# Linear attention at the head of a two-layer kernel: eight products of a constant tile on TensorE before the first k product, finer first loads, and other PSUM banks for the first k and for the split's transposes

## The chip, the cores and the metric

The kernel runs on one core of one Trainium2 chip. The metric is device time in microseconds (us), the median of several executions. Before the change it is 1000.65 us (three executions, 1000.56 to 1001.5). One further execution was profiled; it took 998.07 us, and its span, from the first to the last instruction, is 996.3 us. Durations in this document come from that one execution. Where a line of the kernel is meant, it is written L467 and so on.

TensorE (PE in the profile) multiplies matrices and writes to PSUM, which has eight banks of 128 x 512 f32 here. PEld is the loading of its stationary operand. VectorE is DVE, ScalarE is ACT, GpSimd is POOL, SyncE is SP. "PEq", "SPq" and "ACTq" are the queues in which an engine's instructions, or its DMA issues, stand.

## What is computed

Four blocks run one after the other on 2048 rows of 512 values: a linear attention, a gated feed-forward layer with 4-bit weights, a gated linear attention in chunks, and a feed-forward layer on the rows that a router picks. Each ends in a residual sum and a layer norm. The change is in the first, and in the hand-over to the second:

```python
q = elu(x @ Wq.T) + 1
k = elu(x @ Wk.T) + 1
v = x @ Wv.T                                   # 16 heads of 32
kv = einsum('bhtd,bhte->bhde', k, v)
z = 1.0 / (einsum('bhtd,bhd->bht', q, k.sum(axis=2)) + 1e-06)
out = einsum('bhtd,bhde,bht->bhte', q, kv, z)
x = layernorm(x + out @ Wo.T)
```

## The kernel before

**Tiling.** The 2048 rows are four blocks of 512 (`blk` 0 to 3), two for each of the two sequences (`b`). A block is four row tiles of 128, and the 512 channels are four chunks of 128 (`KC = 4`). All operands of this part are f32; each f32 matmul shows in the trace as two records, so that 16 matmuls of 512 columns are "x32".

**The first k product** (L462 to L470). Four banks, `first[0]` to `first[3]`, collect the k of the four row tiles of block 0. The loop goes over the channel chunk outside and the row tile inside, so that work can begin when the first chunk of `Wk` and of the transposed x has landed. For this the loads at L138 to L141 are issued in chunks: SP issues four loads of `Wk`, ACT five of `x0T`, of which chunk 0 comes in two halves of 256 tokens. Then `elu1` (L265) turns each bank into k: two ACT instructions (L270, L271) that write a buffer `e`, of which there are two, and one DVE instruction (L272) that reads the bank a second time. The bank is free after this last one.

**The other seven products** (`by_seven`, L300). Each later block of k or q is made by a scheme of seven smaller products. It takes one bank from the ring "sum", called `grow`, in which several products accumulate, and two banks from the ring "mm". `by_seven` is a generator; `run` (L480) puts other work between its products: `add_xk` (k transposed times x, which holds four banks of the ring "acc"), `values` and `G_rows` (which turn that into the matrix G), `turned` (a transposed tile of q), `add_o` (that tile times G, added to x by DVE at L448), and for the second sequence `split_some`.

**The split.** `split_quarter` (L207) transposes one normalized row tile of block 0 on TensorE (L196) into a bank, from which ACT copies a rounded part `x1Th` (L210) and DVE subtracts to get the rest `x1Tl` (L211). These are the operands of the second block's first product, `gatep` and `upp` (L621). There are four quarters. The first three come between the products of the last q, the fourth after them, before the last four `add_o`.

**Banks.** `bank(ring, name)` (L88) hands out a ring's banks in turn and counts the turns in `turn_of`. A bank is given again only when its readers are done. To begin with "mm" is banks 0 to 3 and "acc" banks 4 to 7. After the first k product "mm" becomes banks 0 and 1, and "sum" banks 2 and 3 (L471). The ring "acc" serves `add_xk`, `G_rows`, `turned`, `add_o` and the split's transposes.

**Order.** Each engine works through its queue in order. The framework orders the instructions of an engine by when it expects them to be ready, with the program's order behind that; `tc.issue_after(x)` holds what stands in it behind x. `behind()` with `last_pe` (L281 to L285) keeps the matmuls of this part in the program's order. The tile `ones` (L279) is filled by POOL and read much later by `spread_ksum` (L383).

Of the kernel before, what the change touches and what calls it, by code (L numbers as in the profile page):

```python
# [21 lines left out]
P = 128  # L22
B, T, C = 2, 1024, 512
NB = 4
KC = C // P
# [48 lines left out]
def body(ctx: ExitStack, tc: tile.TileContext, a: dict, out: bass.AP):  # L74
    nc = tc.nc
# [7 lines left out]
    dram = ctx.enter_context(tc.tile_pool(name="dram", bufs=1, space=DRAM))  # L83


    rings, turn_of = {"mm": range(4), "acc": range(4, 8)}, {"mm": 0, "acc": 0, "sum": 0}

    def bank(ring, name):  # L88
        i = rings[ring][turn_of[ring] % len(rings[ring])]
        turn_of[ring] += 1  # L90
        return psum.tile([P, 512], F32, tag=f"bank{i}", name=name)

    def mm_bank(name):
        return bank("mm", name)
# [13 lines left out]
    def place_w(i, name):  # L108
        return wpool.tile([P, KC, C], F32, tag=f"A{i}", name=name)

    Wq, Wk, Wv, Wo = (place_w(i, name) for i, name in enumerate(("Wq", "Wk", "Wv", "Wo")))
# [10 lines left out]
    def new_xT(blk):  # L122
        t = xT_slot(blk % 2, f"x0T{blk}")
        return t, a["xT"][:, blk * 512 : (blk + 1) * 512].rearrange("(k p) t -> p k t", p=P)

    def load_xT(blk):
        t, src = new_xT(blk)
        nc.sync.dma_start(out=t, in_=src)
        return t
# [6 lines left out]

    t, src = new_xT(0)
    for k in range(KC):  # L138
        nc.sync.dma_start(out=Wk[:, k], in_=a["WkT"][k * P : (k + 1) * P, :])
        for half in ((slice(0, 256), slice(256, 512)) if k == 0 else (slice(0, 512),)):  # L140
            nc.scalar.dma_start(out=t[:, k, half], in_=src[:, k, half])  # L141
    xT = {0: t}
    load_x(0)
    xT[1] = load_xT(1)
# [47 lines left out]
    def transposed(x, name, room=mm_bank):  # L192

        pt = room(name)
        for k in range(KC):
            ins = nc.tensor.transpose(pt[:, k * P : (k + 1) * P], x[:, k * P : (k + 1) * P], ident).ins  # L196
        last_turned[0] = ins
        return pt

    def split_tiles(blk):  # L200

        i, j = ((2, 2), (1, 0), (0, 1), (2, 2))[blk]
        hi = xT_slot(i, "x1Th", F32R)
        lo = wpool.tile([P, KC, 512], F32R, tag=f"A{j}", name="x1Tl")
        return hi, lo

    def split_quarter(parts, blk, i, room=mm_bank):  # L207
        hi, lo = (t[:, :, i * P : (i + 1) * P] for t in parts)
        pt = transposed(x_t[blk][:, i], "x1Tp", room).rearrange("p (k t) -> p k t", k=KC)
        nc.scalar.copy(hi, pt)  # L210
        nc.vector.tensor_sub(lo, pt, hi.bitcast(F32))  # L211
# [65 lines left out]


    ones = wk.tile([P, P], F32, name="ones", bufs=1)  # L279
    nc.gpsimd.memset(ones, 1.0)  # L280
    last_pe = [None]  # L281

    def behind():

        return ExitStack() if last_pe[0] is None else tc.issue_after(last_pe[0])  # L285

    def new_pair(name):
        return wk.tile([P, 2, C], F32, tag="kq", name=name, bufs=3)
# [3 lines left out]
    def sums_of_weights(w, rooms):  # L292

        B11, B12, B21, B22 = (w[:, 2 * e : 2 * e + 2, 256 * o : 256 * o + 256] for e in range(2) for o in range(2))
        T1, T2, T4 = rooms
        for dst, x, y in ((T1, B12, B11), (T2, B22, T1), (T4, B21, T2), (B12, B22, B12)):
            nc.vector.tensor_sub(dst, x, y)
        return T1, T2, B12, T4
# [54 lines left out]
    tile_of = lambda i: slice(i * P, (i + 1) * P)  # L353
# [49 lines left out]
    vkm_of, qT, parts = {}, {}, []  # L403
# [24 lines left out]
    def turned(blk, i):  # L428
        with behind():
            pt = transposed(pairs_of["q", blk][i // 2][:, i % 2], "qTp", acc_bank)  # L430
        last_pe[0] = last_turned[0]
        t = qT[blk, i] = wk.tile([P, KC, P], F32, tag="qT", name="qT")
        nc.scalar.copy(t.rearrange("p k t -> p (k t)"), pt)

    def add_o(blk, i):

        ao = acc_bank("ao")
        with behind():
            for k in range(KC):
                ins = nc.tensor.matmul(  # L440
                    ao, qT[blk, i][:, k], G_of[blk // 2][:, k], start=k == 0, stop=k == KC - 1
                ).ins
        last_pe[0] = ins
        x = x_t[blk][:, i]
        if i == 0:
            mv_of[blk] = sp.tile([P, 4, 2], F32, tag="mv", name="mv")
        mv = mv_of[blk]
        nc.vector.tensor_add(x, ao, x)  # L448
        row_stats(mv[:, i], x)
        if i == 3 and blk < NB - 1:  # L450
            layernorm(x_t[blk], mv, by=nc.gpsimd)

    def split_some(*part):
        if 0 in part:
            parts.extend(split_tiles(0))
        for i in part:
            with behind():
                split_quarter(parts, 0, i, acc_bank)
            last_pe[0] = last_turned[0]


    pairs_of["k", 0] = [new_pair(f"k{t}") for t in range(2)]  # L462
    first = [mm_bank("kp") for _ in range(4)]
    with behind():
        for k in range(KC):
            for i in range(4):
                ins = nc.tensor.matmul(  # L467
                    first[i], xT[0][:, k, tile_of(i)], Wk[:, k], start=k == 0, stop=k == KC - 1
                ).ins
    last_pe[0] = ins  # L470
    rings["mm"], rings["sum"] = (0, 1), (2, 3)  # L471
    Ts = {"k": sums_of_weights(Wk, slices(Tk, 0, 3))}
    for i in range(4):
        elu1(pairs_of["k", 0][i // 2][:, i % 2], first[i])
# [5 lines left out]
    def run(products, *others):  # L480

        others = list(others)
        for _ in products:
            for step in others.pop(0):
                step()
        for more in others:
            for step in more:
                step()

    def some_xk(blk, *part):  # L490
        return [lambda i=i: add_xk(blk, i) for i in part]

    def turns(blk, *part):
        return [lambda i=i: turned(blk, i) for i in part]

    def some_o(blk, *part):
        return [lambda i=i: add_o(blk, i) for i in part]
# [3 lines left out]
    def k_products(blk):  # L501
        return by_seven(xT[blk], Wk, Ts["k"], S_rooms, pairs_of.setdefault(("k", blk), []), lambda t: sum_k(blk, t))

    def q_products(blk):
        return by_seven(xT[blk], Wq, Ts["q"], S_rooms, pairs_of.setdefault(("q", blk), []), lambda t: weigh(blk, t))
# [3 lines left out]
    for b in range(B):  # L509
        i, j = 2 * b, 2 * b + 1  # L510
        if b:
            run(
                k_products(i),
                turns(1, 0, 1),
                some_o(1, 0) + turns(1, 2) + job(1) + some_o(1, 1) + turns(1, 3) + job(1),
                some_o(1, 2) + job(1), some_o(1, 3) + job(1), job(2),
            )
        run(k_products(j), [], some_xk(i, 0, 1) + job(2), some_xk(i, 2) + job(1), some_xk(i, 3) + job(1), job(1 + b))
        if b == 0:
            Ts["q"] = sums_of_weights(Wq, slices(wdn, 0, 3))  # L520
        else:

            Tq = place_w(1, "Tq")
            for n in range(3):
                nc.scalar.copy(Tq[:, n], wdn[:, n])
            Ts["q"] = (*slices(Tq, 0, 2), Ts["q"][2], *slices(Tq, 2, 3))
            S_rooms[0] = pieces_of(Tq[:, 3])
        run(
            q_products(i), [],
            some_xk(j, 0, 1) + job(1), some_xk(j, 2) + step(spread_ksum, b) + job(1), some_xk(j, 3) + job(1 + b),  # L530
        )
        if b == 0:
            xT[2] = load_xT(2)
        split = [step(split_some, n) if b else [] for n in range(4)]
        run(
            q_products(j),
            step(values, b),
            turns(i, 0, 1) + job(1 - b),
            step(G_rows, b) + split[0] + job(1 - b),
            some_o(i, 0) + turns(i, 2) + split[1] + some_o(i, 1) + turns(i, 3) + job(1 - b),  # L540
            some_o(i, 2) + split[2] + some_o(i, 3),
        )
        if b == 0:
            xT[3] = load_xT(3)
    for more in turns(3, 0, 1) + split[3] + some_o(3, 0) + turns(3, 2) + some_o(3, 1) + turns(3, 3) + some_o(3, 2, 3):
        more()
    late = mv_of[3]
# [17 lines left out]
    free = iter([1, 2, 0] * 4)  # L565
# [27 lines left out]
    with tc.tile_pool(name="s2", bufs=1) as wk2:  # L593
# [198 lines left out]
        for blk in range(NB):  # L792
            h = Hidden(blk)
            for f in range(NI):
# [23 lines left out]
                with tc.issue_after(mm) if blk or f else ExitStack():  # L818
                    mm, st = scaled_sums(f, parts, gate, up, by_three, quarter)
                sl = nc.scalar.activation(gate, gate, AF.Silu).ins  # L820
                hm = nc.gpsimd.tensor_mul(h.chunk(f), up, gate).ins  # L821
                with tc.issue_after(mm), tc.issue_after(st), tc.issue_after(hm), tc.issue_after(sl):
# [7 lines left out]
                    if blk and f in (1, 4, 7):  # L830
                        take(pieces, {1: 22, 4: 32, 7: 24}[f])
                        mm = last_p[0]
# [3 lines left out]
            parts = coming  # L836
# [604 lines left out]
    for blk in range(NB):  # L1441
# [3 lines left out]
        else:  # L1445
            o_sum(blk)
            _, scored = finish(blk - 1)
# [42 lines left out]
    _, xs = fetch(0)  # L1490
# [83 lines left out]
```

## Time and profile before

| what | us |
|---|---|
| median of three executions | 1000.65 |
| the profiled execution | 998.07 |
| its span | 996.3 |
| PE busy in the span | 972.5 |
| DVE busy in the span | 681.1 |
| PE busy in 0 to 250 | 239.87 |
| PE busy in 250 to 500 | 249.93 |
| PE busy in 500 to 750 | 246.85 |
| PE busy in 750 to 1000 (the span ends at 996.3) | 235.83 |
| first matmul starts at | 4.57 |
| first `grow` product starts at | 22.84 |
| fourth quarter of the split starts at | 229.74 |
| second block's first product starts at | 247.28 |

The start times are counted from the start of the span. A row of the waits view gives an instruction group, what ended its engine's idle time, and that time's total, count and longest piece in us. In the timeline a row gives start, duration, engine, line, operation, tiles and, in brackets, the idle time before it and what ended it.

### The profile page before, as it was taken

To read this page: it belongs to the slowest core of one execution; us is meant where nothing else is said; L and a number is where in the kernel's file an instruction comes from. 1 tells how busy PE (TensorE), PEld (TensorE's weight loads), DVE (VectorE), ACT (ScalarE), POOL (GpSimd) and SP (SyncE) were. 2 spreads that over 40 slices of the span, in tenths; PEclk is the share of its full clock that TensorE was granted. 3 is DMA by queue.
4 is the path that set the end of the run, shared out by engine and by line. 5 is a ranking of instruction groups with operands and counts; after the bars stand their busy time and mean duration, and the time that the engine had idled before them with its cause. 6 is when DMAs were issued, how large, how long until landed. Compare 5 with 4: busy or idle time off the path is not lost.

```text
span 996.3 us, 11402 instructions
## 1 busy us (share of the span) xinstructions
PE 972.5 (98%) x4229; PEld 741.8 (74%) x4229; DVE 681.1 (68%) x1290; ACT 288.7 (29%) x490; POOL 302.6 (30%) x277
## 2 busy tenths in 40 slices
PE   7999999998999999999999999999999999999996
PEld 3667666764888888888889665676778688888885
DVE  3558867865995576676664365666798795689644
ACT  2344332342562254245240333122220124220000
POOL 2020363003777445575557022102023012000022
PEclk9999999999999999999999999999999999999999
DMA  9612212200000000000010410000004302140011
GB/s 344 203 47 88 74 62 66 61 1 1 1 1 1 1 1 1 2 11 1 1 58 27 163 59 1 1 1 1 1 22 141 134 11 75 43 169 1 1 43 42
DMA packets 25690, 48.84 MB, mean 49 GB/s; under 512 B 4652, under 2 KB 6316, under 8 KB 25123
## 3 DMA queue, kind: packets, MB, share of 16 engines
q1 hardware_dynamic: 22995, 42.85, 12.9%
q0 software_dynamic: 1920, 4.22, 1.1%
q10 hardware_dynamic: 720, 1.05, 0.3%
q8 instruction: 33, 0.54, 0.2%
q14 instruction: 22, 0.18, 0.1%
HBM read 39.70 MB, written 10.52 MB: 50 GB/s over the span
## 4 chain that ended last, share of the span: by engine, by line
PE 83%; issue 8%; DVE 5%; POOL 2%; ACT 2%; DMA 0%; POOLq 0%; DVEq 0%; ACTq 0%
PE P L668 12%; PE yp L1318 9%; PE hp L1239 9%; PE gatep L621 8%; PE upp L621 8%; PE xk L362 6%; PE ao L440 5%; PE grow L311 5%; PE P L311 3%; PE ao L1122 3%; PE go L1078 2%; PE kp L467 1%; PE lp L584 1%; PE P L677 1%; PE up L995 1%
## 5 line engine op out<-in xcount | busy, mean ns | idle before, releaser
L180 POOL TENSOR_TENSOR rs<-rs,table 128x4 f32<-128x4 f32 (+1 forms) x21 | 18.9, 902 | 328.4 <-DVE rs L179 328.2
L632 DVE SCALAR_TENSOR_TENSOR gate<-gatep,scale,gate 128x512 f32<-128x512 f32 x123 | 91.3, 743 | 7.5 <-PE gatep L621 5.9
L632 DVE SCALAR_TENSOR_TENSOR up<-upp,scale,up 128x512 f32<-128x512 f32 x112 | 83.0, 741 | 0.3
L621 PE MATMUL gatep<-x1Th,wgu 128*128 128x512 f32 x176 | 73.0, 415 | 0.1
L621 PE MATMUL upp<-x1Th,wgu 128*128 128x512 f32 x176 | 69.7, 396 | 0.0
L621 PE MATMUL gatep<-x1Tl,wgu 128*128 128x512 f32 x176 | 69.5, 395 | 0.0
L621 PE MATMUL upp<-x1Tl,wgu 128*128 128x512 f32 x176 | 69.5, 395 | 0.0
L821 POOL TENSOR_TENSOR h<-up,gate 128x512 f32<-128x512 f32 x30 | 38.6, 1288 | 75.9 <-ACT gate L820 70.9
L626 ACT ACTIVATE gate<-gatep,scale 128x512 f32<-128x512 f32 x41 | 28.3, 691 | 113.4 <-PE gatep L621 104.6
L668 PE MATMUL P<-wdn,h 128*128 128x256 f32 x256 | 60.5, 379 | 0.0
L440 PE MATMUL ao<-G,qT 128*128 128x512 f32 x128 | 58.7, 605 | 0.6 <-ACT x1Th L210 0.6
L1122 PE MATMUL ao<-W1o,uT 128*128 128x512 f32 x128 | 55.6, 592 | 0.0
L668 PEld LDWEIGHTS P<-wdn,h 128*128 128x128 f32 x256 | 48.5, 190 | 6.7
L1026 POOL TENSOR_TENSOR sum<-sum,sq 128x512 f32<-128x512 f32 x12 | 19.3, 1606 | 107.6 <-issue 83.7
L1122 PEld LDWEIGHTS ao<-W1o,uT 128*128 128x128 f32 x128 | 24.0, 190 | 28.7 <-issue 27.5
L440 PEld LDWEIGHTS ao<-G,qT 128*128 128x128 f32 x128 | 24.3, 195 | 25.9 <-issue 25.6
L187 DVE BATCH_NORM_STATS2 st<-x 128x6 f32<-128x512 f32 x64 | 42.7, 682 | 0.8
L362 PE MATMUL xk<-pair,x 128*128 128x512 f32 x96 | 42.7, 592 | 0.0
L621 PEld LDWEIGHTS upp<-x1Th,wgu 128*128 128x128 f32 x176 | 33.0, 188 | 9.3 <-DVE up L632 1.1
L621 PEld LDWEIGHTS gatep<-x1Th,wgu 128*128 128x128 f32 x176 | 33.1, 188 | 7.7 <-PE x1Tp L196 0.3
L621 PEld LDWEIGHTS upp<-x1Tl,wgu 128*128 128x128 f32 x176 | 33.1, 188 | 7.5
L621 PEld LDWEIGHTS gatep<-x1Tl,wgu 128*128 128x128 f32 x176 | 33.1, 188 | 7.2 <-issue 0.2
(403 smaller groups left out, 2231.6 us busy)
## 6 DMA issues: line engine op xcount, KB each, us to landing
pk<-in_gu SPq DMA_DIRECT2D x16, 352.0 KB, 3.7
x<-in_x SPq DMA_DIRECT2D x4, 1024.0 KB, 12.8
w<-in_w SPq DMA_DIRECT2D x1, 4096.0 KB, 14.4
xs<-picked SPq DMA_DIRECT2D x4, 1024.0 KB, 5.1
out<-x SPq DMA_DIRECT2D x4, 1024.0 KB, 4.3
w<-in_w SPq DMA_DIRECT2D x4, 1024.0 KB, 7.6
x0T<-in_xT SPq DMA_DIRECT2D x3, 1024.0 KB, 6.9
pk<-in_dn SPq DMA_DIRECT2D x11, 256.0 KB, 3.4
```

The source lines that it names most:

```text
L187: nc.vector.bn_stats(st, x)
L311: ins = nc.tensor.matmul(ps[:, 256 * r : 256 * r + 256], a[:, k, r * P : (r + 1) * P], b[:, k], start=first and r == 0 and k == 0, stop=k ...
L362: ins = nc.tensor.matmul(acc_of[b][c], x_t[blk][:, i, c * P : (c + 1) * P], pairs_of["k", blk][i // 2][:, i % 2], start=blk % 2 == 0 and i ...
L440: ins = nc.tensor.matmul(ao, qT[blk, i][:, k], G_of[blk // 2][:, k], start=k == 0, stop=k == KC - 1).ins
L621: ins = nc.tensor.matmul(ps, wgu[:, k, at * P : (at + 1) * P], x[:, k], start=x is parts[0], stop=x is parts[1]).ins
L626: nc.scalar.activation(acc, ps, AF.Copy, scale=s)
L632: last = nc.vector.scalar_tensor_tensor(acc, ps, s, acc, ALU.mult, ALU.add).ins
L668: last_p[0] = nc.tensor.matmul(cut, x(j)[:, r], w[:, j], start=j == 0, stop=j == NP - 1 and tail is None).ins
L821: hm = nc.gpsimd.tensor_mul(h.chunk(f), up, gate).ins
L1122: nc.tensor.matmul(ao[i], uT[blk][:, k, i * P : (i + 1) * P], W1o[:, k], start=n == 0, stop=n == 3)
L1239: nc.tensor.matmul(ps[:, 256 * j : 256 * j + 256], w[:, k, 2 * g + j], x[:, k], start=k == 0, stop=k == 1)
L1318: nc.tensor.matmul(ps[:, 256 * r : 256 * r + 256], x(r, j), w(j), start=j == 0, stop=j == NJ - 1)
```

## The change

The first chunk of `Wk` is loaded in two halves of 256 output channels, and the first chunk of `x0T` in parts of 128, 128 and 256 tokens. DVE fills `ones` in place of POOL. Eight 128 x 128 products of `ones` with itself are put on TensorE into one bank of the ring "acc"; nothing reads them, and the first k product is kept behind them. The first k product uses banks 4, 5, 1 and 3 in place of 0, 1, 2 and 3, and for chunk 0 each of its matmuls is two of 256 columns. After it, the turns of the ring "mm" begin at 0 again. The first three quarters of the split take the "sum" bank that the last q's `grow` does not use, in place of a bank of the ring "acc", and the fourth quarter takes a bank of the ring "mm".

```diff
-    rings, turn_of = {"mm": range(4), "acc": range(4, 8)}, {"mm": 0, "acc": 0, "sum": 0}
+    rings, turn_of = {"mm": range(4), "acc": range(4, 8)}, {"mm": 0, "acc": 0, "sum": 0, "free": 0}
...
     for k in range(KC):
-        nc.sync.dma_start(out=Wk[:, k], in_=a["WkT"][k * P : (k + 1) * P, :])
         for half in ((slice(0, 256), slice(256, 512)) if k == 0 else (slice(0, 512),)):
-            nc.scalar.dma_start(out=t[:, k, half], in_=src[:, k, half])
+            nc.sync.dma_start(out=Wk[:, k, half], in_=a["WkT"][k * P : (k + 1) * P, half])
+        for part in ((slice(0, 128), slice(128, 256), slice(256, 512)) if k == 0 else (slice(0, 512),)):
+            nc.scalar.dma_start(out=t[:, k, part], in_=src[:, k, part])
...
     ones = wk.tile([P, P], F32, name="ones", bufs=1)
-    nc.gpsimd.memset(ones, 1.0)
-    last_pe = [None]
+    nc.vector.memset(ones, 1.0)
+
+    idle = bank("acc", "idle")
+    for _ in range(8):
+        ins = nc.tensor.matmul(idle[:, :P], ones, ones, start=True, stop=True).ins
+    last_pe = [ins]
...
             with behind():
-                split_quarter(parts, 0, i, acc_bank)
+                split_quarter(parts, 0, i, lambda name: bank("free", name))
...
     pairs_of["k", 0] = [new_pair(f"k{t}") for t in range(2)]
+    rings["mm"] = (4, 5, 1, 3)
     first = [mm_bank("kp") for _ in range(4)]
     with behind():
         for k in range(KC):
             for i in range(4):
-                ins = nc.tensor.matmul(
-                    first[i], xT[0][:, k, tile_of(i)], Wk[:, k], start=k == 0, stop=k == KC - 1
-                ).ins
+                for o in (slice(0, 256), slice(256, 512)) if k == 0 else (slice(0, 512),):
+                    ins = nc.tensor.matmul(
+                        first[i][:, o], xT[0][:, k, tile_of(i)], Wk[:, k, o],
+                        start=k == 0 and o.start == 0, stop=k == KC - 1, skip_group_check=True,
+                    ).ins
     last_pe[0] = ins
-    rings["mm"], rings["sum"] = (0, 1), (2, 3)
+    rings.update(mm=(0, 1), sum=(2, 3))
+    turn_of.update(mm=0)
...
         split = [step(split_some, n) if b else [] for n in range(4)]
+        rings["free"] = (rings["sum"][(turn_of["sum"] + 1) % 2],)
         run(
             q_products(j),
...
+    rings["free"] = rings["mm"]
     for more in turns(3, 0, 1) + split[3] + some_o(3, 0) + turns(3, 2) + some_o(3, 1) + turns(3, 3) + some_o(3, 2, 3):
         more()
```

## The prediction

> **What bounds the kernel now.** I read the page's busy times first, then all waits of TensorE, then the chain that ended last for the first 300 us, and then the timeline around each wait.
>
> ```profile
> PE 972.5 (98%) x4229; PEld 741.8 (74%) x4229; DVE 681.1 (68%) x1290; ACT 288.7 (29%) x490; POOL 302.6 (30%) x277
> ```
>
> TensorE has work in 98% of the span, so nearly all of the remaining time is in its few waits. The waits view names the ones that the change can touch:
>
> ```profile
> PE kp L467 <- DMA x0T<-in_xT: 4.6, 1, 4.6
> PE x1Tp L196 <- DVE x1Tl L211: 2.6, 1, 2.6
> PE grow L311 <- DVE k L272: 2.3, 1, 2.3
> PE ao L440 <- ACT x1Th L210: 0.6, 1, 0.6
> ```
>
> The reader is to see that these are four single events, not repeated ones. Between 24.84 and 215.40 the chain is TensorE alone, piece after piece, so a microsecond won at the start arrives at 215 whole. The waits show only half of the loss, though. The timeline of the weight loads shows TensorE's pace, since each load follows the record before it:
>
> ```profile
> 7.29 0.34 PEld L467 LDWEIGHTS kp<-Wk,x0T 128*128 128x128 f32 x1 [0.52 <-issue]
> 8.14 0.34 PEld L467 LDWEIGHTS kp<-Wk,x0T 128*128 128x128 f32 x1 [0.52 <-issue]
> 8.80 0.19 PEld L467 LDWEIGHTS kp<-Wk,x0T 128*128 128x128 f32 x1 [0.32 <-issue]
> 9.23 0.19 PEld L467 LDWEIGHTS kp<-Wk,x0T 128*128 128x128 f32 x1 [0.24 <-issue]
> ...
> 232.87 0.34 PEld L440 LDWEIGHTS ao<-G,qT 128*128 128x128 f32 x1 [0.52 <-issue]
> 233.72 0.27 PEld L440 LDWEIGHTS ao<-G,qT 128*128 128x128 f32 x1 [0.52 <-issue]
> 234.22 0.19 PEld L440 LDWEIGHTS ao<-G,qT 128*128 128x128 f32 x1 [0.24 <-issue]
> ```
>
> Starts lie 0.855 us apart up to 8.14 and 0.43 apart from 8.80. The step of 0.66 between holds 0.46 at the slow pace, so the change of pace is at about 8.6. The same slow pace is there again after the wait at 229.74, and ends at about 233.9. Around that second wait the timeline reads:
>
> ```profile
> 226.87 0.24 PE L552 MATMUL pg<-table,sg 88*128 88x88 f32 x1
> 229.06 0.63 DVE L211 TENSOR_TENSOR x1Tl<-x1Tp,x1Th 128x512 fp32r<-128x512 f32 x1
> 229.74 0.66 PE L196 MATMUL x1Tp<-table,x 128*128 128x128 f32 x4 [2.63 <-DVE x1Tl L211]
> 230.20 0.68 DVE L448 TENSOR_TENSOR x<-ao,x 128x512 f32<-128x512 f32 x1
> 231.03 5.08 PE L440 MATMUL ao<-G,qT 128*128 128x512 f32 x8 [0.63 <-ACT x1Th L210]
> 235.94 0.60 PE L196 MATMUL qTp<-table,pair 128*128 128x128 f32 x4
> ```
>
> Quarter 3 of the split stands in the bank of quarter 2, whose subtraction DVE reaches only at 229.06, although ACT copied it at 222.77: DVE is busy without a gap from 218.46. Then the product takes 4.91 us to the next start, where the same eight records take 3.43 elsewhere in the chain.
>
> **What the Trainium skill says.** "TensorE: Matmul & The Clock Gate", Part 1 (The HAM clock gate): TensorE runs at half rate by default and after idling, and goes to full rate after a busy window of about 3.4 us; the window is free-running. The trace agrees: the pace halves exactly, and 8.6 and 233.9 are 66.0 windows of 3.413 us apart. "PSUM — Partial Sum Buffer", PSUM bank collisions, asks to guard PSUM by bank, not by address; so a late reader holds the whole bank, as at 229.74. The same page, The four PSUM rules, says that a first matmul clears a bank's accumulate bits as a whole, so the two halves of chunk 0 need one `start` only; no trace here shows it. "DMA: Bandwidth & Descriptors", Issuing engines are not separate DMA queues: SP's and ACT's loads share the engines and interleave. The trace agrees: 0.75 of all DMA time is in use in 2 to 4 us with both issuing.
>
> **Part 1, the front.** The first product now needs 128 x 256 of Wk and 128 x 128 of x: with the interleaved neighbour part some 256 KB. DMA windows of 0.25 us before (74, 29, 147, 266, 299, 291 GB/s and so on from 1.75) sum to 276 KB at 3.25 and 512 KB at 4.1. Before, both queues' first 256 KB were needed, and the release came at 4.53, 0.4 after that point; so now the data should be there at about 3.7. But the eight products stand ahead. They can start at 0.71 (POOL's memset start) + 0.20 (its duration) + 0.05 = 0.96. No row shows a 128-column f32 product at the slow pace. Nearest is vk (L412): 32 records, 16 products, in 3.57 us, 0.223 each; twice that for the slow pace is 0.446, and eight are 3.57. They end at 4.53. So the start is won not at all (4.53 against 4.57), and the smaller loads are hidden behind the products. The clock is what is won: with windows where they lay before, 1.77 to 5.19 is now a busy one, and the slow pace ends at 5.19. It costs (5.19 - 4.53)/2 = 0.33 in place of (8.6 - 4.57)/2 = 2.0. Gain 1.7. Bounds: if a half-busy window suffices, the products go faster and data decides: 0.87 + 2.0 = 2.9. If the loads and streams of the products don't overlap (0.34 + 0.21 each at the slow pace, half after 5.2), they end at about 7.6: a loss of 1.0. I take 1.7 since loads overlap in vk.
>
> Chunk 0 as 16 records of 256 columns in place of 8 of 512: the `P` row of L311 takes 1.73 for 8, 0.216 each, so nothing is added; the extra loads (0.19, or 0.34 slow) lie beside records as long as they. SP and ACT each issue one DMA more (0.42 and 0.46). Before, ACT's fifth and SP's fifth DMA waited until 4.5 and 4.35, as if eight could be in flight; now the third and fourth chunks fall under this wait. With 5 to 6.6 us to landing they are there at about 10; chunk 2 is used at 4.53 + 0.3 + 2 x 3.43 = 11.7 and chunk 3 at 15.1. Hidden; without that cover a microsecond each. x of block 0, which queues on SP behind them (landing 17.2 before), is first used at 22. The memset costs DVE 0.2 while it has nothing else.
>
> **Part 2, the first k's banks.** The last kp record starts at 19.96 (its group ends at 20.55, and a record's latency is 0.592), and `grow` could follow at 20.39. It waits to 22.84 for bank 2, until DVE has made k of row tile 2. Its successor starts at 24.68, and without the wait at 20.39 + 1.73 = 22.12. Gain 2.5. Afterwards bank 2 and bank 0 are unused, so both products follow at once. What is late next: add_xk, 3.46 after kp's end, needs k of tiles 0 and 1 (0.2 and 0.8 after it, from 20.71 and 21.31 against 20.55) and banks 4 to 7, of which 4 and 5 come free by the same two instructions. xT of block 1 landed at 14.6; `grow` now comes at about 18.7. The DVE sum of Wq at 22.70 needs a load that lands at about 21.6 and may hold back k of tile 3; its reader comes some 17 us later. Bounds 2.3 to 2.6.
>
> **Part 3, the split's banks.** Quarter 3 goes to bank 1, last read at 219.06 (L346), and may follow pg at 227.0. Its four transposes take 0.43. The ring "acc" is shifted by one for the unread products and loses the splits' turns, so add_o of tile 0 gets the bank of block 2's tile 2, read at 224.35. It starts at 227.41 at full pace and ends at 230.84. The next transpose's bank was block 2's tile 3, whose read (L448) begins at 230.20 and ends at 230.88; it starts at 230.93 in place of 235.94. Gain 5.0: 2.63 + 0.63 waits, 1.5 slow pace, 0.2 slow transposes. Quarters 0 to 2 share one bank, with 4 us and more from a subtraction to the next quarter. What is late next is that read, by 0.1 only. Bounds: without the second slow pace in an ordinary execution (the window falls differently) 3.5; with the DVE read behind the fourth subtraction and row statistics (0.69 + 0.69 + 0.18) about 3.4; 5.1 at best.
>
> **Sum.** 1.7 + 2.5 + 5.0 = 9.2 us. From the profiled 998.07 that gives 988.9; the span falls from 996.3 to 987.1. The median lies 2.6 above the profiled time, which I keep: 1000.65 - 9.2 = 991.5. After 242 the second block is bound by TensorE and its operands are ready, so nothing gives this back.
>
> **Rivals.** (a) The wait at the split moves rather than goes: DVE is the bound from 218 to 231, and its order there may change. For: no gap in its timeline, 0.1 slack. Against: its old order suffices. With a gain of 2 there: 994.5. (b) The eight products don't bring the clock up in time, or run longer than estimated. For: window position is free, and no trace shows such products. Against: TensorE is busy without a gap from 0.96. With no gain in part 1: 993.2. (c) The slower side: DVE's in-order queue puts the memset behind the first sums of the weights and of xT (5.42 to 16.6). Then the products run from 16.8 to 20.4, kp ends at 34.1, and `grow` comes 11.3 late; less 5.0 at the split: 1007. It decides once the memset ends after 10.3, where a loss of 7.5 in the front eats parts 2 and 3. Against: POOL's memset was ordered to 0.71, ahead of copies that wait for the table. (d) Other bank numbers later (the rings are rebuilt at L788 and L843) shift small waits by a microsecond or two, either way.
>
> **How the numbers follow.** The forecast has 0.55; its own range is 990 to 993. (a) has 0.17, (b) 0.15, (c) 0.03, (d) with larger losses than said 0.10, of which half still ends under 998.6. A measurement of this kernel can tell 0.2%, about 2 us, from no change. So faster 0.92, same 0.05, slower 0.03. The range 989.3 to 996.3 takes in (a), (b) and the bounds of parts 1 and 3.
>
> **What would show it.** Right: products from about 1.0 to 4.5, kp's records at 0.43 by 5 to 7 us, no wait before the first `grow`, no wait over 0.5 at the split's fourth quarter and no record pace of 0.855 around 231; the second block's first product at about 238. Wrong: a late memset, first kp well after 4.6, or a new wait of TensorE on L448 or L211 near 222 to 230.

## The result and the profile after

The changed kernel takes 989.44 us in the median of four executions (988.88 to 990.65), against 1001.01 us for the kernel before beside it (four executions, among them the three of 1000.65). The ratio is 0.9886, with a 95% interval of 0.9869 to 0.9903. The profiled execution went from 998.07 to 988.88 us, its span from 996.3 to 987.1 us.

Lines of the changed kernel are numbered a few higher: L474 is L467 before, L316 is L311, L197 is L196, L212 is L211, L445 is L440 and L453 is L448; in some experiments they shift by a few more.

In the view of all waits, these are TensorE's in the changed kernel (waiter, line, releaser; then us in total, count, longest):

```profile
PE dp L989 <- DVE last L974: 1.5, 2, 1.2
PE ep L942 <- ACT l L931: 1.3, 1, 1.3
PE hp L1250 <- ACT row L1218: 1.1, 1, 1.1
PE idle L285 <- DVE ones L281: 1.0, 1, 1.0
PE rp L1163 <- DVE score L1146: 0.9, 1, 0.9
PE kp L474 <- DMA x0T<-in_xT: 0.3, 1, 0.3
PE mp L1043 <- POOL sum L1037: 0.3, 1, 0.3
```

The three waits of the attention part (x1Tp 2.6, grow 2.3, ao 0.6) are gone, and the wait for the first data is 1.0 for the constant tile instead of 4.6 for x. One wait is new: kp for x, 0.3. The others belong to later stages and were there before with the same sizes.

The timeline of TensorE in the changed kernel at the start:

```profile
1.04 3.64 PE L285 MATMUL idle<-ones 128*128 128x128 f32 x16 [1.04 <-DVE ones L281]
4.51 1.89 PE L474 MATMUL kp<-Wk,x0T 128*128 128x256 f32 x8
6.73 12.29 PE L474 MATMUL kp<-Wk,x0T 128*128 128x256 f32 x32 [0.33 <-DMA x0T<-in_xT]
18.86 1.89 PE L316 MATMUL grow<-Wk,x0T 128*128 128x256 f32 x8
20.59 1.89 PE L316 MATMUL P<-Wk,x0T 128*128 128x256 f32 x8
```

kp begins at 4.51, right behind the eight products (the listed end of a group overlaps the start of the next, here as in other rows), and kp's first eight records, of 256 columns, take 1.73 us at full pace before the wait. The new wait stands before the other 32: row tiles 2 and 3 need the third part of x. `grow` follows kp at once, and so does `P`, the second product of `by_seven`. And around the split's fourth quarter:

```profile
222.78 0.60 PE L197 MATMUL x1Tp<-table,x 128*128 128x128 f32 x4
223.22 3.67 PE L445 MATMUL ao<-G,qT 128*128 128x512 f32 x8
...
224.97 0.63 DVE L212 TENSOR_TENSOR x1Tl<-x1Tp,x1Th 128x512 fp32r<-128x512 f32 x1
...
226.11 0.68 DVE L453 TENSOR_TENSOR x<-ao,x 128x512 f32<-128x512 f32 x1
...
226.85 0.66 PE L197 MATMUL qTp<-table,pair 128*128 128x128 f32 x4
```

The fourth quarter starts at 222.78, although the third's subtraction only starts at 224.97. The next transpose, at 226.85, comes right behind the read at 226.11 to 226.79: now that read is the last to arrive, with next to no wait.

A reckoning by starts, in the two profiled executions:

| place | before | after | won in all | won in this part |
|---|---|---|---|---|
| end of kp, where `grow` could start | 20.39 | 18.86 | 1.53 | 1.5 (front) |
| second product of by_seven | 24.68 | 20.59 | 4.09 | 2.6 (first k's banks) |
| transpose after the fourth quarter | 235.94 | 226.85 | 9.09 | 5.0 (split's banks) |
| span | 996.3 | 987.1 | 9.2 | |

So the profiled gain is 9.2 us and comes from where the prediction had put it. But the median fell by 11.6. Two questions were left: which part carries the missing 2.4 us, and why x came late in kp.

### The profile page after: what moved, and what is told of

Read it like the earlier page. It is cut to its first block, busy times and chain, and to the rows that moved or that the text cites. A ratio compares the mean times of both kernels' runs of the same rounds, so it can differ in the third digit from the quotient of the medians.

```text
span 987.1 us, 11453 instructions
## 1 busy us (share of the span) xinstructions
PE 972.1 (98%) x4253; PEld 745.1 (75%) x4253; DVE 683.3 (69%) x1291; ACT 288.4 (29%) x490; POOL 300.2 (30%) x276
## 4 chain that ended last, share of the span: by engine, by line
PE 84%; issue 8%; DVE 4%; POOL 2%; ACT 1%; DMA 1%; POOLq 0%; ACTq 0%; DVEq 0%
PE P L679 12%; PE yp L1329 9%; PE hp L1250 9%; PE gatep L632 8%; PE upp L632 8%; PE ao L445 6%; PE xk L367 6%; PE grow L316 5%; PE P L316 4%; PE ao L1133 3%; PE go L1089 2%; PE lp L595 1%; PE P L688 1%; PE kp L474 1%; PE up L1006 1%
## 5 line engine op out<-in xcount | busy, mean ns | idle before, releaser
L445 PE MATMUL ao<-G,qT 128*128 128x512 f32 x128 | 57.3, 593 | 0.0
L445 PEld LDWEIGHTS ao<-G,qT 128*128 128x128 f32 x128 | 23.8, 190 | 24.3 <-issue 23.9
```

What stands on the lines that cost most here:

```text
L445: ins = nc.tensor.matmul(ao, qT[blk, i][:, k], G_of[blk // 2][:, k], start=k == 0, stop=k == KC - 1).ins
```

## Experiments

Four kernels first, each the changed one with one part undone.

### The split's banks undone

```diff
-                split_quarter(parts, 0, i, lambda name: bank("free", name))
+                split_quarter(parts, 0, i, acc_bank)
```

> The changed kernel with the split's transposes back in the ring acc. Theory (the split's bank holds TensorE, and the idle time also halves its pace): the wait of x1Tp on DVE x1Tl of about 2.6 us is back at the fourth quarter, with some records 0.855 apart behind it; the distance from the last q's side product to the second block's first product is 3.3 to 5.0 us longer than in the changed kernel (5.0 if the pace halves, 3.3 if not), so a span of 990.4 to 992.1. Rival (the gain at the split came from the earlier order of DVE, not from the bank): no wait over 1 us there, span 987 to 988.5.

Measured: median 995.89 us (993.13 to 996.54), ratio to before 0.9958 (0.9943 to 0.9972), profiled span 993.9. The span is above the expected one since kp had a wait of 2.0 us for x in this execution; `grow` came at 20.37. At the split, TensorE's timeline and then its weight loads:

```profile
227.17 0.66 PE L197 MATMUL x1Tp<-table,x 128*128 128x128 f32 x4 [2.63 <-DVE x1Tl L212]
...
228.50 0.50 PE L632 MATMUL gatep<-x1Th,wgu 128*128 128x512 f32 x1 [0.68 <-ACT x1Th L211]
228.84 5.29 PE L445 MATMUL ao<-G,qT 128*128 128x512 f32 x8
...
233.97 0.60 PE L197 MATMUL qTp<-table,pair 128*128 128x128 f32 x4
```

```profile
229.27 0.29 PEld L445 LDWEIGHTS ao<-G,qT 128*128 128x128 f32 x1 [0.24 <-issue]
230.07 0.34 PEld L445 LDWEIGHTS ao<-G,qT 128*128 128x128 f32 x1 [0.52 <-issue]
230.93 0.34 PEld L445 LDWEIGHTS ao<-G,qT 128*128 128x128 f32 x1 [0.52 <-issue]
...
232.63 0.24 PEld L445 LDWEIGHTS ao<-G,qT 128*128 128x128 f32 x1 [0.52 <-issue]
233.11 0.19 PEld L445 LDWEIGHTS ao<-G,qT 128*128 128x128 f32 x1 [0.24 <-issue]
```

The wait is back at its old size, 2.63, and behind it the records are 0.855 us apart for some 3.4 us. The transpose comes at 233.97; with the front's 1.51 taken off it is 5.6 later than in the changed kernel, of which some 0.6 is work that stands earlier in the order here (`pg` and the first `gatep`). The rival, an earlier order of DVE, falls.

### The first k's banks undone

```diff
-    rings["mm"] = (4, 5, 1, 3)
+    rings["mm"] = (0, 1, 2, 3)
```

> The changed kernel with the first k product in banks 0 to 3 again. Theory: grow waits for DVE's third k instruction, 2.3 us again, and its successor comes 2.5 us later than in the changed kernel; span about 989.6. Rival (with the front's other edits the bank is free sooner, or add_xk would have waited anyway): under 1.5 us, span under 988.6.

Measured: median 993.79 us (992.44 to 994.46), ratio to before 0.994 (0.9916 to 0.9964), span 992.2. That is 5.1 us of span, not 2.5. The timeline of TensorE shows why:

```profile
22.14 3.17 PE L316 MATMUL grow<-Wk,x0T 128*128 128x256 f32 x8 [2.34 <-issue]
25.10 2.42 PE L316 MATMUL P<-Wk,x0T 128*128 128x256 f32 x8
27.36 1.02 PE L367 MATMUL xk<-k,x 128*128 128x512 f32 x2
```

The wait is 2.34 (the view names no releaser; DVE's third k instruction runs from 21.35 to 22.04). But `grow` and `P` take 2.96 and 2.26 to the next start where 1.73 is usual, so 1.8 us are lost to half pace, for a wait of the same size that had no such sequel in the profile of before. The granted clock that the trace records agrees: from 22 to 26 it is 0.59 here and 1.00 in the profile of before. The front cost another 0.8 here: kp's first eight records took 2.42 in place of 1.89, and then it waited 0.47 for x.

### No products, and the old loads

```diff
-    for _ in range(8):
-        ins = nc.tensor.matmul(idle[:, :P], ones, ones, start=True, stop=True).ins
-    last_pe = [ins]
+    last_pe = [None]
```

> The changed kernel without the eight unread products, finer loads kept. Theory (the products only bring the clock up, and hide the finer loads): the first k record starts at 3.2 to 3.8, runs at 0.43 for each half record (half pace) until 3.4 to 6.8 us after it, and the first grow comes 0.6 to 2.4 us later than in the changed kernel, so 19.5 to 21.3. Rival (the finer loads are what wins, the products cost as much as they bring): grow within 0.4 us of 18.86, or earlier.

Measured: median 990.64 us (990.44 to 990.87), ratio 0.9912 (0.989 to 0.9935). TensorE's timeline begins with kp:

```profile
3.56 3.78 PE L472 MATMUL kp<-Wk,x0T 128*128 128x256 f32 x8 [3.56 <-DMA x0T<-in_xT]
7.68 12.57 PE L472 MATMUL kp<-Wk,x0T 128*128 128x256 f32 x32 [0.34 <-DMA x0T<-in_xT]
```

The first eight records take 3.78 at half pace, a wait of 0.34 for x follows, and `grow` comes at 20.09, as expected. So the finer loads do bring the first data a microsecond earlier, and the slow pace eats it. The products were worth 1.2 us against this profile of the changed kernel; against its second profile, shown further below, in which `grow` comes at 20.33, they were worth nothing.

```diff
-            nc.sync.dma_start(out=Wk[:, k, half], in_=a["WkT"][k * P : (k + 1) * P, half])
-        for part in ((slice(0, 128), slice(128, 256), slice(256, 512)) if k == 0 else (slice(0, 512),)):
+        nc.sync.dma_start(out=Wk[:, k], in_=a["WkT"][k * P : (k + 1) * P, :])
+        for part in ((slice(0, 256), slice(256, 512)) if k == 0 else (slice(0, 512),)):
```

> The changed kernel with the first chunk's loads as before (Wk whole, x in two halves of 256 tokens), products kept. Theory (the finer loads are hidden behind the products): first k record at 4.5 to 4.7 and grow within 0.3 us of 18.86; the 0.33 us wait for x at 6.4 is smaller or gone, since its second half is issued earlier. Rival (finer loads carry part of the gain): grow 0.5 us or more later than 18.86.

Measured: median 989.01 us (988.42 to 989.55), ratio 0.9897 (0.9874 to 0.9919), span 986.8. TensorE's timeline has one piece for kp, with no wait:

```profile
1.04 3.62 PE L284 MATMUL idle<-ones 128*128 128x128 f32 x16 [1.04 <-DVE ones L280]
4.63 14.02 PE L473 MATMUL kp<-Wk,x0T 128*128 128x256 f32 x40
18.49 1.89 PE L315 MATMUL grow<-Wk,x0T 128*128 128x256 f32 x8
```

`grow` comes 0.37 us sooner than at 18.86, a little outside the expected 0.3 and on the other side from the rival. The finer loads are not merely hidden; between these two executions they cost 0.4 us.

### Is it the idling that halves the pace?

Here the kernel before keeps its loads, its banks and both waits; only, TensorE multiplies `ones` in the waits.

```diff
+    def fill(i, n):
+        ps = psum.tile([P, 512], F32, tag=f"bank{i}", name="fill")
+        for _ in range(n):
+            with behind():
+                last_pe[0] = nc.tensor.matmul(ps[:, :P], ones, ones, start=True, stop=True).ins
+
+    fill(7, 10)
     rings["mm"], rings["sum"] = (0, 1), (2, 3)
...
         for i in part:
+            if i == 3:
+                fill(1, 12)
             with behind():
```

> The kernel before, with unread 128-column products of ones put into its two later waits: ten (about 2.2 us at full pace) in front of the first grow and twelve (2.6 us) in front of the split's fourth quarter; loads, banks and front as before. Theory (a wait of some 2.6 us costs a second time, because the pace halves for up to 3.4 us after it in those executions where a clock window falls into it): the waits stay in size, but no records 0.855 us apart behind 20 us; the profiled span is 1.0 to 2.5 us shorter than the 996.3 of before, the median 1 to 3 us below that of the kernel before, and the executions lie closer together than the 4 us of before. Rival (slow records at 231 are due to their operands or banks, not to idling): the slow records stay, median within 0.5 us of before or later.

Measured: median 996.87 us (996.17 to 997.88), against 1000.44 (997.52 to 1001.54) for the kernel before beside it; ratio 0.9967 (0.9954 to 0.9979). The profiled span, 996.0, is a miss against the expected 1.0 to 2.5 below 996.3: this execution ran at half pace until about 10.5 at its start, in place of 8.6, which puts kp's end and everything up to the split 1.0 us later. The waits kept their size: `grow` comes 2.46 after kp's end (2.45 before), released by DVE's k, and the fourth quarter again comes right behind DVE's subtraction.

```profile
23.85 1.59 PEld L311 LDWEIGHTS grow<-Wk,x0T 128*128 128x128 f32 x8 [0.26 <-DVE k L272]
...
230.75 0.66 PE L196 MATMUL x1Tp<-table,x 128*128 128x128 f32 x4
...
232.04 3.67 PE L440 MATMUL ao<-G,qT 128*128 128x512 f32 x8 [0.55 <-ACT x1Th L210]
```

The wait of `ao` behind the quarter is still there (0.55), and its eight records take 3.67 in place of 5.08, which wins 1.4. From 230 to 234 the granted clock is 1.00; in the profile of before it is 0.57. (At the start of every profile it reads 1.00, although the records there run at half pace, so for the start only the distance of the records counts.) The median fell by 3.6, more than the expected 1 to 3, and the executions lie 1.7 apart against 4.0. The rival, operands or banks, falls.

This bears on the median. The spans of the kernel before that were taken beside the experiments lie in two groups. Beside the first four kernels, seven are 995.8 to 996.9 us with a mean granted clock of 0.996, and five are 998.5 to 1000.0 with 0.993 or 0.994. A mean lower by 0.003 over 1000 us is 6 us at half pace, or 3 us lost, which is the distance of the groups. This reckoning is rough, since the mean also counts the end of the span, where the clock is at half behind TensorE's last record and costs nothing (from about 991.6 in the profile of before). The profile of the kernel before, 996.3 at 0.996, is one of the first group. No profile of the second group was kept; that its lost time lies behind the two waits is inferred from the fillings, which took it away. How many executions fall into the second group differs between sets, so the median of the kernel before is 998.64, 999.76, 1000.44 or 1001.01.

The same question at the split alone, with the loads of the best kernel below:

```diff
         for i in part:
+            if i == 3:
+                fill = psum.tile([P, 512], F32, tag="bank1", name="fill")
+                with behind():
+                    for _ in range(12):
+                        last_pe[0] = nc.tensor.matmul(fill[:, :P], ones, ones, start=True, stop=True).ins
             with behind():
-                split_quarter(parts, 0, i, lambda name: bank("free", name))
+                split_quarter(parts, 0, i, acc_bank)
```

> The loads of the kernel with x in two halves, the split's transposes in the ring acc as before, and twelve unread products of ones in front of its fourth quarter. The wait stays, only TensorE doesn't idle in it. Theory (the split's bank costs about 3.3 us of waiting and the rest, 1.5 to 3, by the halved pace): median 3.0 to 4.0 us above the kernel with x in two halves, no records 0.855 apart near 230. Rival (the wait alone costs all of it): 5 to 6.5 us above.

Measured: median 992.87 us (991.91 to 993.19), 3.8 above the same kernel with the free bank (989.05, below); spans 990.1 and 986.7, 3.4 apart. Undone without the filling it had cost 5.4 to 6.4 in the median, against 990.52 and 989.44 for the two sets of the changed kernel. So at the split the wait is worth 3.4 to 3.8. The rest, 1.6 to 3.0, is put down to pace: the traces show 1.4 to 1.7 of it in one execution, and what lies above that rests on comparing sets that were not taken beside each other.

### How many products, and which parts of x

```diff
-    for _ in range(8):
+    for _ in range(4):
```

> The changed kernel with four unread products in place of eight; they end at about 2.8 us, and data for the first k is there at about 3.6. Theory (a window has to be busy nearly in full): the first k records start at 3.5 to 3.8 at half pace, and the pace doubles at 4.4 to 7.5 us; grow at 18.5 to 20.5. Rival (half a window of work suffices): full pace at the latest by 5 us in each such execution, grow no later than in the changed kernel but for the wait for the third part of x.

Measured: median 990.24 us (988.95 to 990.77), ratio 0.9896 (0.9877 to 0.9915). The products end at about 2.8, kp starts at 3.57, and its eight records take 3.75: half pace until 7 us at least, in spite of the work from 1.04 on. So here work with a gap of 0.45 us before kp did not bring the pace up in time, and `grow` came at 20.26. That only unbroken work raises it does not follow. Without the products, above, the pace rose at about 8.2, close behind an idle gap of 0.34 at 7.34 to 7.68: from 7.68 to `grow` it took 12.41 us, where the changed kernel takes 12.13 from the same record, and 0.28 lost is 0.56 at half pace. How much idling is too much stays open.

```diff
-        for part in ((slice(0, 128), slice(128, 256), slice(256, 512)) if k == 0 else (slice(0, 512),)):
+        for part in ((slice(0, 128), slice(128, 512)) if k == 0 else (slice(0, 512),)):
```

> The changed kernel with the first chunk of x in two parts, 128 and 384 tokens, in place of 128, 128 and 256. Theory (the third part lands late because the ACT queue, with rows of 512 bytes against 1 and 2 KB on the SP queue, gets the smaller share of the DMA engines, and because it is issued a place later): the rest of x lands before 6.4, no wait over 0.2 us in kp, grow at 18.3 to 18.6. Rival (the landing is set by the total of bytes in flight, whatever the parts): a wait of 0.3 to 2 us again, in front of row tile 1 or 2.

Measured: median 990.28 us (988.9 to 991.07), ratio 0.9896 (0.9877 to 0.9915). Neither came out. kp waited 0.60 for x already before its first record, at 5.42, and the half pace went on until about 9, again with a gap in the work; `grow` came at 21.12.

```diff
-        for part in ((slice(0, 128), slice(128, 256), slice(256, 512)) if k == 0 else (slice(0, 512),)):
+        for part in ((slice(0, 256), slice(256, 512)) if k == 0 else (slice(0, 512),)):
```

> The changed kernel with the first chunk of Wk in halves but the first chunk of x in two halves of 256 tokens, as before. Same question: theory gives no wait over 0.2 us in kp and grow at 18.3 to 18.6, rival a wait of 0.3 to 2 us in front of row tile 2.

Measured: median 988.44 us (988.33 to 988.73), ratio 0.9882 (0.9865 to 0.99), no wait in kp, `grow` at 18.32. Only x differs from the changed kernel. The changed kernel and this one again, beside each other on one chip:

> The changed kernel once more, beside the next two on one chip, to have another of its executions. Theory (its finer loads of x cost a wait that differs from one execution to the next): a wait of 0.3 to 2 us for x in kp in this profile too, executions 1.5 us or more apart. Rival (the one profile was an exception): no such wait, and a median within 0.3 us of the kernel with x in two halves.

> The kernel with Wk's first chunk in halves and x in two halves of 256 tokens, against the changed kernel on the same chip. Theory: no wait in kp, median 0.5 to 1.5 us below the changed kernel, executions within 1 us. Rival: equal.

Measured: the changed kernel 990.52 us (989.49 to 990.87; ratio 0.9906, 0.9889 to 0.9924), with x in two halves 989.05 (988.31 to 989.78; ratio 0.9894, 0.9874 to 0.9914), beside 999.76 for the kernel before. Of the changed kernel's two expected signs, the wait came and the spread did not reach 1.5. With halves the median lies 1.5 lower, as expected, but the executions, expected within 1 us, also lie 1.5 apart. So a wait that differs between profiles is shown, and a smaller spread with halves is not. The timelines of TensorE, first of the changed kernel, then with two halves:

```profile
4.62 2.90 PE L474 MATMUL kp<-Wk,x0T 128*128 128x256 f32 x8
8.20 12.29 PE L474 MATMUL kp<-Wk,x0T 128*128 128x256 f32 x32 [0.68 <-DMA x0T<-in_xT]
20.33 1.89 PE L316 MATMUL grow<-Wk,x0T 128*128 128x256 f32 x8
```

```profile
4.51 13.92 PE L474 MATMUL kp<-Wk,x0T 128*128 128x256 f32 x40
18.27 1.89 PE L316 MATMUL grow<-Wk,x0T 128*128 128x256 f32 x8
```

In this second profile the changed kernel's kp begins at half pace, then waits 0.68, and `grow` comes at 20.33, against 18.86 in the first. Whenever x began with a part of 128 tokens (rows of 512 bytes), kp waited for x at least once after TensorE had begun, 0.3 to 2.0 us in all seven profiles. In the four profiles with products and halves of 256 it did not, but for a weight load that waited 0.16 us in the kernel with the old loads. The guess that the ACT queue gets the smaller share of the DMA engines with short rows did not hold for the kernel with two parts, and the traces speak against it: from 3 to 5 us all DMA engines together moved 128 to 230 GB/s in those seven profiles, and 299 to 328 GB/s in the six with halves, the kernel before and its filled form among them. So it is the whole flow that is slower then, not ACT's share of it. Why stays open.

## Why the prediction was right, and where it was not

**Part 2, the first k's banks.** Predicted 2.5, measured 2.56 in the profiles. k of the first tiles and banks 4 and 5 were in time, as said. In ordinary executions it is worth more: undoing it cost 3.3 to 4.4 us of median, against the two sets of the changed kernel, and its profile shows 1.8 of half pace beside the wait.

**Part 3, the split's banks.** Predicted 5.0, measured 5.0, in an execution before that had one slow stretch at the split. The next to arrive late is the read by L453 that the prediction named, within 0.1 us. The second block's first product on the new quarters came at 238.12, where about 238 had been forecast. The bound "without the second slow pace in an ordinary execution (the window falls differently) 3.5" fits the wait alone, 3.4 to 3.8. What it did not weigh right is the other direction: ordinary executions of the kernel before lose more to half pace than the profiled one.

**Part 1, the front.** Predicted 1.7, measured 1.5 in the profile, by other terms. The products did end at about 4.5 and the first record did start there. The pace rose at about 4.4 and not at 5.19, which brought 0.3 more. Then "the smaller loads are hidden behind the products" failed: the third part of x landed late, and the first of the 32 records came 0.5 us after the eight before it were through (6.73 in place of 4.51 + 1.73 = 6.24). The prediction had looked at the third and fourth channel chunks, which were in time, and took the first chunk's third part for granted. In the second profile kp's end came at 20.33, so the front won less than 0.1 there, against the 20.39 of the profile before. That the first profile came within 0.2 of the forecast is therefore luck. With x in two halves behind the products, kp's end lies at 18.1 to 18.5 in four profiles.

**Sum.** 9.2 predicted and 9.2 measured in span. In the median 991.5 was forecast and 989.44 measured, outside the prediction's narrower range of 990 to 993. The step that failed is "The median lies 2.6 above the profiled time, which I keep". That distance is no constant that the change leaves alone. It goes when TensorE is kept busy in the two waits, so it was half pace behind them, in those executions in which a clock window fell into them. The change takes it away too, so the median fell by 11.6. After the change the median lies 0.6 above its profiled execution, and 0.1 in the second set. The size of the fall depends on the set: in the second one it is 9.2, from 999.76 to 990.52. The wide range held the first result by 0.1 only (989.44 against a low end of 989.3), so there is luck in that too.

**Rivals.** (a) fell, the old DVE order sufficed. (b) is true of some executions: in the second profile kp's first eight records took 2.90 in place of 1.89, so the pace rose only at about 6.6. (c) did not come: the memset ran at 0.82. (d) left no trace beyond the reckoning above.

## What to carry to other kernels

A wait of TensorE of two or three microseconds had two prices here: itself, and up to 1.8 us of half pace after it, and not every execution paid the second; so a median above the profiled time may be such a loss rather than an offset. Where a wait can't be removed, unread products in it took away the second price. With products ahead of the first data, the products set the start of the first real one, and finer loads had nothing left to win. Such products paid where the data was there when they ended: with x in two halves kp's end came at 18.1 to 18.5, against 20.4 and 21.4 in the two profiles with neither products nor finer loads. With x in finer parts they did not always pay. A kernel that differs from the one with halves by the products alone was not run.

## What was not expected

The kernel before has two groups of executions, 3 us apart, that go with a mean granted clock of 0.996 or 0.993 to 0.995. Keeping TensorE busy in its two waits, without shortening them, took 3.6 us off the median, although TensorE's busy time rose from 972.5 to 977.0 us.

The pace at the start can rise 3.4 us after the first product (changed kernel) or 5.8 after it (the kernel before with fillings). The free-running window of the Trainium skill ("TensorE: Matmul & The Clock Gate", Part 1), about 3.4 us long, allows both. With the split's banks undone it rose sooner still. There kp began at 4.34, against 4.62 in the changed kernel's second profile, whose products all ran at half pace; the 0.28 between them puts the rise at about 4.05 (an estimate from these starts), 3.0 after the first product. With a window of that length, some 0.4 us of it had been idle. So a window need not be full, and what the four products showed is only that theirs, in that execution, was not full enough.
